# A two-layer graph kernel: two basis products in 15 block products, a root and an output product in seven

## The chip, the cores and the metric

The kernel runs on one core of a Trainium2 chip. The core has a matrix engine (TensorE, "PE" in the profile, with its weight loads as "PEld"), a vector engine (VectorE, "DVE"), an activation engine (ScalarE, "ACT"), a general engine (GpSimd, "POOL"), and queues that start transfers between main memory and the core's own memory (the one used most is that of SyncE, "SP"). Products land in PSUM, which has eight banks of 128 x 512 float32; VectorE and ScalarE read them from there. The metric is the device time of one execution in microseconds (us), as the median of the runs.

## The reference

Two graph blocks follow each other on 384 nodes with 1024 features. The first is an attention block with an edge mask; the change leaves it alone. The second is a relational convolution in two layers, with 768 features inside:

```python
h = relu(layernorm(x))                       # x is the output of the attention block
f = relu(h @ w_in + b_in)                    # 384 x 768
for l in range(2):
    W = einsum('rb,bio->rio', comp[l], basis[l])   # 6 relations out of 4 bases, 768 x 768 each
    h_all = einsum('ni,rio->rno', f, W)
    agg = segment_sum(h_all[edge_type, src] * norm[:, None], dst)   # mean by relation and node
    f = batchnorm(relu(agg + f @ root[l] + conv_bias[l]) + f)
x = x + layernorm(f @ w_out + b_out) * ln_gamma + ln_beta
```

The kernel writes the sum over edges as products with count matrices. With A_r the 384 x 384 matrix of relation r (counts divided by their sums), and At_b = sum over r of comp[r, b] A_r, a layer is: sum over b of At_b (f basis_b), plus f root, plus the bias.

## The kernel before

All matrices are float32, in tiles of 128 partitions. A float32 matmul shows as two instructions in the trace. The work of the second block runs in this order, and each step has a name in the profile.

- **Input product** (`ps_x`, `multiply`, L402): f = relu(h w_in), held as `XT`, six feature tiles by 384 nodes. It is done by a seven-product scheme (Winograd's form of Strassen's): the matrices are cut in quarters, VectorE makes four sums of each, and seven quarter products stand for eight. Every scheme named below works that way: fewer matmuls, paid with sums of operands and with results that are read out of PSUM and added.
- **Bases** (`ps_g`, L985 and L979, the loop over `b`): for every basis, H_b = f basis_b, 384 x 768. Node blocks 0 and 1 go by seven products, node block 2 directly. That is 33 matmuls with 384 columns, or 66 instructions. VectorE makes the sums of the weights (`weight_sums`, L927 and L929; `last_sums`, L935) and of f (`node_sums`, L920), ScalarE copies first results to `H`, and VectorE adds second ones (L992, L1000, L1002). The last product of a basis (`rest`) is issued inside the next.
- **Counts and mixes** (`share`, L361 to L367; `mix`, L346 and L348): GpSimd counts the edges into tables with indirect transfers (L283), loads them as `A` (L850 to L854) and adds them up (L355, L356). `share` makes a division by the sums, and `mix` forms `At`. A dictionary, `between`, fixes by (layer, basis, step) where these stand: in layer 0 at bases 2 and 3 and at the root, in layer 1 at its bases.
- **Root** (`ps_c`, L1019): f root, directly, 36 matmuls with 384 columns, accumulated in six banks to which the first mixed product is added.
- **Mixed product and normalisation** (`ps_c`, L1077): the sum over b of At_b H_b as seven-product schemes, in three pairs of feature tiles. For each pair VectorE makes four sums of `H` (`feature_sums`, L1097), adds seven results to `XN` (`take`, L1107), and makes the batch norm (`measure`, L1042 to L1049, `normalise_layer`, L1054 to L1058).
- **Output product** (`ps_f`, L1183): f w_out, directly, one node block after another. Then come the row norm (L1187 to L1195), the addition of x (L1197) and the store (L1198). GpSimd has by then added ln_beta to x (L1170).

The order on TensorE, VectorE, GpSimd, SP and, from the second product on, ScalarE is the order of the program, since all of these engines are scheduled by hand. Each engine takes its instructions strictly in that order, so an instruction that waits holds up those behind it. SP issues the loads of weights in that order too. Weights use five buffers in turn (`wpool`, 768 KB each): a load waits until the fifth load before it has been used up.

Of the kernel before, what the change touches and what calls it, by code (L numbers as in the profile page):

```python
# [10 lines left out]
F32 = mybir.dt.float32  # L11
# [6 lines left out]
P = 128  # L18
# [10 lines left out]
HC = DC // 2  # L29
HN = N // 2  # L30
# [14 lines left out]

BQ, BK, BV, BIQ, BIK, BIV, B_IN, CB, GAM, BET, NCOL = 0, 8, 16, 24, 32, 40, 48, 54, 66, 78, 90
# [5 lines left out]
def gnn_kernel(ctx: ExitStack, tc: tile.TileContext, out, x, edges, chunks, cols, rows, small,  # L52
               wq, wk, wv, wiq, wik, wiv, wo, w_in, basis, root, w_out):
# [299 lines left out]
    def add_up(r):  # L353
        sums[r] = late.tile([P, N], F32, tag="sum", name="sum", bufs=4)
        nc.gpsimd.tensor_tensor(sums[r], A[:, r, 0, :], A[:, r, 1, :], ALU.add)  # L355
        nc.gpsimd.tensor_tensor(sums[r], sums[r], A[:, r, 2, :], ALU.add)  # L356

    def share(r):
# [3 lines left out]
        rn = late.tile([P, N], F32, tag="rn", name="rn", bufs=2)  # L362
# [9 lines left out]
    with ExitStack() as inner:  # L372
# [263 lines left out]
        A = late.tile([P, R, NT, N], F32, tag="A", name="A")  # L636

# [93 lines left out]
        for g in range(STEPS + 1):  # L731
# [14 lines left out]
            if f + 2 == STEPS:  # L746
# [4 lines left out]
                w_first = [wload(basis[0, 0, part], (2, DC), "w_c") for part in range(3)]  # L751
                w_first += [wload(basis[0, 1, part], (2, DC), "w_c") for part in range(2)]
# [117 lines left out]
        node_sum(T, 4, h2T, T4)  # L870
        rest = lambda: None
        for p in range(3):
# [13 lines left out]
            add_up_quad(quads[0][0], pb)  # L886
            multiply(pc, s[:, 0], T[1], True)
# [8 lines left out]
            if p == 0:  # L896
                output_sums(a[2], S[0])

# [7 lines left out]
    with tc.tile_pool(name="conv", bufs=1) as cp:  # L906
# [7 lines left out]

        def node_sums(X):
            S = cp.tile([P, 4, 3, P], F32, tag="S", name="S")
            for i, a, b, op in ((0, block(X, 1, 0), block(X, 1, 1), ALU.add), (1, S[:, 0], block(X, 0, 0), ALU.subtract),
                                (2, block(X, 0, 0), block(X, 1, 0), ALU.subtract),
                                (3, block(X, 0, 1), S[:, 1], ALU.subtract)):
                nc.vector.tensor_tensor(S[:, i], a, b, op)  # L920
            return S

        def weight_sums(w):
            T13 = keep.tile([P, 3, 2, HC], F32, tag="hT", name="T13")
            T2 = keep.tile([P, 3, HC], F32, tag="mask8", name="T2")
            for c in range(3):
# [5 lines left out]
        def last_sums(w, T2):  # L932
            T4 = cp.tile([P, 3, HC], F32, tag="T4", name="T4")
# [4 lines left out]
        w_first = [w_first[:3], w_first[3:]]  # L938

        def load_basis(l, b):  # L940
            w = w_first.pop(0) if w_first else []
# [328 lines left out]
```

## Time and profile before

| what | value |
|---|---|
| time, median of 3 runs | 715.99 us (715.83 to 717.43) |
| the profiled execution's own time | 717.47 us |
| its span in the trace | 715.7 us |
| granted TensorE clock, mean | 0.995 |
| PE busy | 699.9 us, 98% |
| PEld busy | 527.9 us, 74% |
| DVE busy | 512.6 us, 72% |
| POOL busy | 308.1 us, 43% |
| ACT busy | 157.6 us, 22% |

The span runs from the first to the last instruction of the trace; some 1.8 us of the execution's own time lie around it. The busy share of PE is of a pipelined engine and says only that it is seldom without work. A group of the profile reads: line, engine, operation, output <- inputs, partitions x elements, count, then busy time and mean nanoseconds of one, then idle time of the engine before it and what ended it. In a list in order of time the columns are start, length and what ran.

### The profile page before, as it was taken

The numbers are of one execution on the slowest core, as the hardware profiler recorded it, in microseconds if no ns is written. First come the engines' busy times: TensorE is split into PE (matmuls) and PEld (weight loads), VectorE is DVE, ScalarE is ACT, GpSimd is POOL, SyncE is SP. The second block draws the span as 40 slices with busy tenths as digits, with TensorE's granted clock in tenths as the row PEclk, the third lists the DMA queues.
The fourth block names the chain that finished last, engine by engine and source line by source line (L and its number), as shares of the span: only waits on it lengthen the run. The fifth ranks groups of instructions, "written<-read, shape, count | busy, mean of one in ns | idle before, by whom it ended". The sixth has DMA issues, their size and how long they took to land.

```text
span 715.7 us, 9149 instructions
## 1 busy us (share of the span) xinstructions
PE 699.9 (98%) x3228; PEld 527.9 (74%) x3228; DVE 512.6 (72%) x1307; ACT 157.6 (22%) x360; POOL 308.1 (43%) x239
## 2 busy tenths in 40 slices
PE   8999999999999999999999999999999999999995
PEld 7759999999997444478985555558975555579943
DVE  5886697868886699787534279798878766507756
ACT  3211111111111577410221124202131111011100
POOL 1366777778687788687786542000000000120000
PEclk9999999999999999999999999999999999999999
DMA  8788787373562622733424994311104322700001
GB/s 303 267 279 264 228 250 212 80 243 67 203 209 43 177 2 1 221 44 45 89 0 103 250 288 153 133 44 45 45 0 133 102 69 94 308 1 1 1 30 59
DMA packets 69180, 91.04 MB, mean 127 GB/s; under 512 B 22940, under 2 KB 50688, under 8 KB 68750
## 3 DMA queue, kind: packets, MB, share of 16 engines
q1 hardware_dynamic: 46830, 78.45, 32.6%
q0 software_dynamic: 21296, 9.60, 10.8%
q10 hardware_dynamic: 1008, 2.41, 0.9%
q8 instruction: 25, 0.41, 0.2%
q14 instruction: 21, 0.17, 0.1%
HBM read 79.27 MB, written 11.16 MB: 126 GB/s over the span
## 4 chain that ended last, share of the span: by engine, by line
PE 87%; DVE 10%; ACT 2%; DMA 1%; issue 0%; DVEq 0%; ACTq 0%
PE ps_g L985 12%; PE ps_g L979 10%; PE ps_k L402 10%; PE ps_c L1077 10%; PE ps_v L402 8%; PE ps_q L420 6%; PE ps_q L402 5%; PE ps_f L1183 4%; DVE At L348 4%; PE ps_y L402 3%; PE ps_c L1019 3%; PE ps_x L402 3%; PE ps_o L707 2%; PE ps_s L662 2%; PE ps_pT L696 2%; PE ps_v L586 2%
## 5 line engine op out<-in xcount | busy, mean ns | idle before, releaser
L283 POOL DMA_INDIRECT atab<-count,at x99 | 166.3, 1679 | 44.2 <-issue 23.5
L278 POOL DMA_INDIRECT mtab<-m_val,at x99 | 103.4, 1045 | 57.6 <-issue 22.9
L1170 POOL TENSOR_TENSOR x_sb<-x_sb,room 128x1024 f32<-128x1024 f32 x3 | 7.0, 2348 | 188.9 <-DMA room<-in_rows 188.9
L348 DVE SCALAR_TENSOR_TENSOR At<-A,small_sb,At 128x1152 f32<-128x1152 f32 x40 | 53.6, 1414 | 0.0
L979 PE MATMUL ps_g<-T,S 128*128 128x384 f32 x144 | 49.1, 486 | 0.0
L985 PE MATMUL ps_g<-w_c,XN 128*128 128x384 f32 x144 | 47.7, 487 | 1.1 <-DVE XN L1107 1.1
L985 PE MATMUL ps_g<-w_c,XT 128*128 128x384 f32 x144 | 47.9, 486 | 0.0
L420 PE MATMUL ps_q<-hT,w_q 128*128 128x384 f32 (+1 forms) x160 | 43.4, 435 | 1.4 <-DVE hT L108 1.4
L985 PEld LDWEIGHTS ps_g<-w_c,XN 128*128 128x128 f32 x144 | 27.3, 190 | 20.2 <-DVE XN L1107 1.4
L979 PEld LDWEIGHTS ps_g<-T,S 128*128 128x128 f32 x144 | 27.3, 190 | 19.2 <-ACT H L991 0.4
L985 PEld LDWEIGHTS ps_g<-w_c,XT 128*128 128x128 f32 x144 | 27.3, 190 | 18.8
L420 PEld LDWEIGHTS ps_q<-hT,w_q 128*128 128x128 f32 x160 | 30.1, 200 | 14.1 <-ACT hT L101 1.7
L1077 PE MATMUL ps_c<-At,H 128*128 128x192 f32 x216 | 36.4, 326 | 0.0
L1077 PEld LDWEIGHTS ps_c<-At,H 128*128 128x128 f32 x216 | 35.4, 190 | 0.5
L402 PE MATMUL ps_k<-T,S 128*128 128x192 f32 x192 | 35.1, 326 | 0.0
L1107 DVE TENSOR_TENSOR XN<-XN,ps_c 128x192 f32<-128x192 f32 x38 | 12.5, 349 | 30.8 <-ACT XN L1063 19.7
L402 PEld LDWEIGHTS ps_k<-T,S 128*128 128x128 f32 x192 | 31.8, 190 | 0.0
L1183 PE MATMUL ps_f<-w_out,XN 128*128 128x512 f32 (+1 forms) x84 | 31.1, 531 | 0.0
L675 DVE CUSTOM_DVE_ANT_0 s<-ps_s,mask 128x384 f32<-128x384 f32 x48 | 24.5, 550 | 5.3 <-PE ps_s L662 5.3
L267 DVE SCALAR_TENSOR_TENSOR same<-cells,own,later 128x128 f32<-128x128 int32 x99 | 28.0, 350 | 0.4
L267 DVE SCALAR_TENSOR_TENSOR same<-keys,key,weigh 128x128 f32<-128x128 int32 x99 | 27.9, 349 | 0.0
L1183 PEld LDWEIGHTS ps_f<-w_out,XN 128*128 128x128 f32 x84 | 15.9, 190 | 14.9 <-issue 14.3
(298 smaller groups left out, 1411.6 us busy)
## 6 DMA issues: line engine op xcount, KB each, us to landing
w_c<-in_basis SPq DMA_DIRECT2D x96, 192.0 KB, 4.1
atab<-zero SPq DMA_DIRECT2D x36, 192.0 KB, 5.2
A<-atab POOLq DMA_DIRECT2D x12, 576.0 KB, 9.0
keys<-keys_d SPq DMA_DIRECT2D x25, 192.0 KB, 5.1
w_c<-in_root SPq DMA_DIRECT2D x6, 768.0 KB, 7.1
w_q<-in_wiq SPq DMA_DIRECT2D x16, 256.0 KB, 6.4
w_k<-in_wk SPq DMA_DIRECT2D x16, 256.0 KB, 5.8
w_k<-in_wik SPq DMA_DIRECT2D x16, 256.0 KB, 3.0
```

The source lines that it names most:

```text
L267: nc.vector.scalar_tensor_tensor(same, row[:, n, :], mine[:, c:c + 1], times, ALU.is_equal, ALU.mult, accum_out=count[:, i, c:c + 1])
L278: nc.gpsimd.indirect_dma_start(mtab[c // PER][:, :], bass.IndirectOffsetOnAxis(at[:, 0, c:c + 1], 0), m_val[:, c:c + 1], None)
L283: nc.gpsimd.indirect_dma_start(atab[0 if i < 11 else i % 2][:, :], bass.IndirectOffsetOnAxis(at[:, 1, c:c + 1], 0), count[:, 1, c:c + 1], ...
L348: nc.vector.scalar_tensor_tensor(At[:, b], A[:, r], w, At[:, b], ALU.mult, ALU.add)
L402: nc.tensor.matmul(ps, a[:, k, :], b[:, k, :], start=start and k == 0, stop=(k == 3), skip_group_check=not start)
L420: nc.tensor.matmul(ps[o][:, c], wt_[:, k, o * P:(o + 1) * P], src[:, k, c], start=(k == 0 and c.start == 0), stop=(k == KD - 1 and c.stop ...
L675: nc.vector.tensor_tensor_reduce(s[j], ps[:, :N], mask8[:, t, :], -scale, 3.0e38, ALU.add, ALU.min, tops[:, j:j + 1])
L979: nc.tensor.matmul(ps, x[:, c], y(c), start=start and c == 0, stop=(c == 2), skip_group_check=not start)
L985: nc.tensor.matmul(ps, block(XT, n, i)[:, c], w[c][:, i, o * HC:(o + 1) * HC], start=(first and c == 0), stop=(c == 2 and (i == 1 or ps is ...
L1019: nc.tensor.matmul(pr[o], w[k // 2][:, k % 2, o * P:(o + 1) * P], XT[:, k, :], start=(k == 0), stop=(k == KC - 1))
L1077: nc.tensor.matmul(ps, x[:, c], y[:, c], start=start and c == 0, stop=stop and c == 5, skip_group_check=True)
L1183: nc.tensor.matmul(p, XT[:, k, t * P:(t + 1) * P], w[k // 2][:, k % 2, c0:c1], start=(k == 0), stop=(k == KC - 1))
```

## The change

It has five parts.

1. **Bases 0 and 1 of layer 0** no longer go through the loop over `b`. `bases_by_15` cuts f in six blocks (three node blocks by two halves of the features) and the basis in six (two by three thirds of 256 outputs), and makes H with 15 block products where 18 would stand; a product is three matmuls with 256 columns. `X_SUMS` lists 11 sums of f, made once for both bases; `W_SUMS` lists 10 sums of each basis; `PRODUCTS` lists the order, the PSUM chain (0 to 3) on which a product accumulates, and the outputs to which the chain is put after it, with a sign. The first to reach an output is a ScalarE copy, later ones are VectorE additions. Sums stand some three products ahead of their use. The two bases are loaded in thirds (`thirds`), and room for sums is taken in `At`, `x_all`, `room2`, `mroom` and `w_room`.
2. **Sums for basis 2**: `weight_sums` of its parts 0 and 1 stand at the products 7 and 8 of basis 1, `node_sums` at its product 13, part 2 behind the last product. The loads stand at products 10 and 14 of basis 0 and 8 of basis 1.
3. **Root of layer 1** goes by seven products in three pairs of feature tiles (`second_root`), 63 matmuls with 192 columns. Its results go through PSUM to `XN` by ScalarE copies and VectorE additions, and the first mixed products are added from banks of their own. The sums of f stand at (1, 3, 1), the first sums of the root at (1, 3, 2).
4. **Output product**: node blocks 0 and 1 by seven products with 512 columns, block 2 directly as before. The sums of w_out stand ahead of the mixed product of layer 1 and inside its pairs (`out_sums`). `finish` makes the row norm; for block 0 and half of block 1 it uses ScalarE and GpSimd and stores from SP.
5. **The addition of ln_beta to x** moves from GpSimd at the end to VectorE in the input product, with a load on SP behind the first five loads of bases.

```diff
+W_SUMS = (
+    (6, 1, 2, 1, 5, -2),
+    (7, 1, 1, 1, 6, -1),
+    (8, 1, 4, 1, 7, 0),
...
+PRODUCTS = (
+    (2, 1, 0, ((4, 1),)),
+    (6, 6, 1, ((7, 1), (8, -1))),
+    (7, 7, 0, ((7, 1),)),
+    (5, 8, 2, ((7, 1),)),
+    (9, 9, 1, ((6, -1),)),
+    (10, 10, 0, ((8, -1),)),
+    (3, 4, 3, ((4, 1),)),
+    (11, 5, 0, ((5, -1),)),
+    (12, 12, 3, ((3, -1),)),
...
+                for b, t in ((0, 2), (0, 1), (0, 0), (1, 2), (1, 1)):
+                    load_third(b, t)
+                nc.sync.dma_start(boB, rows[R_LNB:R_LNB + 1, :].to_broadcast([P, D]))
...
+            for t in {1: (0,), 2: (1, 2)}.get(p, ()):
+                nc.vector.tensor_tensor(x_sb[:, t, :], x_sb[:, t, :], boB, ALU.add)
...
+        def bases_by_15():
+            todo = [(g * NPROD + w[5], 1, g, i) for g in range(BY_15) for i, w in enumerate(W_SUMS) if g or i > 1]
...
+            todo += [(first[x[0]] - 3, 2, 0, i) for i, x in enumerate(X_SUMS) if x[0] not in (6, 14)]
+            todo = sorted(todo + [(NPROD + 13, 3, 0, 0)] + [(NPROD + k, 4, 0, c) for c, k in enumerate((7, 8))])
+            for step in range(NPROD * BY_15):
+                g, k = step // NPROD, step % NPROD
+                while todo and todo[0][0] <= step:
+                    _, kind, *what = todo.pop(0)
+                    if kind == 1:
+                        sum_weights(*what)
+                    elif kind == 2:
+                        sum_features(what[1])
+                    elif kind == 3:
+                        third.append(node_sums(XT))
+                    else:
+                        third.append(weight_sums(basis_loads, what[1]))
...
+                for j in range(3):
+                    nc.tensor.matmul(ps, x[:, j], w[:, j], start=start and j == 0, stop=(j == 2),
+                                     skip_group_check=not start)
+                for to, sign in targets:
...
+                    if (g, to) in begun:
+                        nc.vector.tensor_tensor(dst, dst, ps, ALU.add if sign > 0 else ALU.subtract)
+                    elif sign > 0:
+                        nc.scalar.copy(dst, ps)
+                    else:
+                        nc.scalar.activation(dst, ps, AF.Identity, scale=-1.0)
...
+                if (g, k) == (0, 7):
+                    load_third(1, 0)
+                elif (g, k) in ((0, 10), (0, 14), (1, 8)):
+                    basis_loads.append(wload(basis[0, len(basis_loads)], (2, DC), "w_c"))
...
+        def second_root(rest):
+            root_w.append(wload(root_thirds[2], (KC, HC2), "w_c"))
...
+            shares_ = share_sums()
+            for p in range(3):
...
+                times(pa, root_block(p, 0, 0), x_quarter(0, 0), True)
+                nc.scalar.activation(quads[0][0], pa, AF.Identity, bias=bs[0])
+                rest()
+                times(pb, root_block(p, 0, 1), x_quarter(1, 0), True)
+                nc.vector.tensor_tensor(quads[0][0], quads[0][0], pb, ALU.add)
+                times(pc, s[:, 0], T[0], True)
+                nc.scalar.activation(quads[1][1], pc, AF.Identity, bias=bs[1])
+                if p < 2:
+                    root_S.append(root_sums(p + 1))
+                times(pa, s[:, 1], T[1])
...
+                w_end = [wload(w_out[part], (2, D), "w_out") for part in range(3)]
...
+                out_sums((0, 0), (1, 0), (0, 1), (1, 1))
...
             pa = first_of(0)
+            if l:
+                rest()
...
                 times(pa, S[p][1], T2)
                 take(o0, 1, pa)
                 next(sums, None)
+                if l + 1 == L:
+                    out_sums(*(((0, 2), (1, 2), (2, 2), (3, 2)) if last else ((2, p),)))
                 times(pc, S[p][3], q(1, 1))
...
                 ready = measure(rectify(o1))
                 pa = following
+                if l + 1 == L:
+                    out_sums((3, p))
...
-        for t in range(NT):
-            nc.gpsimd.tensor_tensor(x_sb[:, t, :], x_sb[:, t, :], rowsB[:, 2, :], ALU.add)
...
+        third(*parts[0], 0, 1)
+        times(pa, block(XT, 0, 0), b_end(0, 0), True)
+        put_out(0, 0, pa, True, False)
+        times(pb, block(XT, 0, 1), b_end(1, 0), True)
+        put_out(0, 0, pb, False, True)
+        times(pc, OS[0], summed(0), True)
...
+        times(pa, OS[2], summed(2))
+        finish(0)
+        put_out(1, 0, pa, False, True)
+        put_out(1, 512, pa, False, True)
+        third(*parts[0], *range(2, KC))
+        for p, c0 in parts[1:]:
+            third(p, c0, *range(KC))
+        finish(1)
+        for p, c0 in parts:
+            put_out(2, c0, p, True, True)
+        finish(2)
```

## The prediction

> **What bounds the kernel now.** I read the page's shares first, then the chain that ended last in order of time, then the costs by shape, then single stretches of VectorE.
>
> ```profile
> PE 699.9 (98%) x3228; PEld 527.9 (74%) x3228; DVE 512.6 (72%) x1307; ACT 157.6 (22%) x360; POOL 308.1 (43%) x239
> PEclk9999999999999999999999999999999999999999
> ```
>
> TensorE is hardly ever without work, at a granted clock of 0.995. Only fewer or shorter matmuls, or the ends of the span, can bring time.
>
> ```profile
> 332.45 3.45 PE ps_y L840 x16
> 341.11 2.60 PE ps_x L402 x16
> 368.91 0.37 DVE XT L882
> 370.89 11.61 PE ps_g L985 x36
> 459.46 26.58 DVE At L348 x20
> 616.99 19.35 PE ps_c L1019 x60
> 677.29 30.94 PE ps_f L1183 x84
> 708.26 0.43 DVE hf L1187
> ```
>
> The chain is PE nearly throughout, so its pieces give the price of a matmul instruction: 384 columns 11.61/36 = 0.3225 us, 256 columns 3.45/16 = 0.2156, 192 columns 2.60/16 = 0.1625. The output product is 60 instructions with 512 columns and 24 with 256: (30.94 - 24 x 0.2156)/60 = 0.4295. Per column that is 0.838 to 0.846 ns, so narrower matmuls lose nothing here. One stretch of the chain is VectorE's: the mixes of layer 0 (26.58 us).
>
> **What TensorE saves.** A float32 matmul is two instructions.
> - Bases 0 and 1: before 2 x 66 x 0.3225 = 42.57 us; after 2 x 15 x 3 x 2 = 180 x 0.2156 = 38.81. Saves 3.76.
> - Root of layer 1: before 72 x 0.3225 = 23.22; after 3 x 7 x 3 x 2 = 126 x 0.1625 = 20.48. Saves 2.74. The four first mixed products remain.
> - Output: before 30.94; after 7 x 3 x 2 = 42 x 0.4295 = 18.04 and block 2 as before, 12 x 0.4295 + 24 x 0.2156 = 10.33. Saves 2.57.
>
> Together 9.07 us. The rest of the working is how much of that VectorE takes back.
>
> **Bases 0 and 1.**
>
> ```profile
> L927 DVE TENSOR_TENSOR T<-w_c 128x768 f32<-128x768 f32 x15 | 14.3, 952 | 0.0
> L929 DVE TENSOR_TENSOR T<-w_c,T 128x384 f32<-128x384 f32 x15 | 8.4, 558 | 0.5
> L1187 DVE TENSOR_TENSOR hf<-ps_f,room 128x256 f32<-128x256 f32 x2 | 0.8, 424 | 2.8 <-PE ps_f L1183 2.8
> ```
>
> A sum of weights has 768 elements (0.95 us; 0.87 from start to start where nothing depends on the one before), a sum of f 384 (0.56; 0.47), an addition out of PSUM 256 (0.42). In the 30 products VectorE has 18 sums of weights (two stand earlier), 9 of f, 20 additions, and for basis 2 two weight parts of 1.46 us and four node sums (2 us): 18 x 0.92 + 9 x 0.50 + 20 x 0.40 + 2.9 + 2 = 34 us, against 38.8 of PE. Nearly full, so order decides. I laid both queues side by side from 370.9, product by product (1.29 us each), with 0.15 us from a product's end to its reader. All sums are in time by 1.5 us or more, since they stand three products ahead. Late are the banks: the sums of steps 4 to 6 (three of weights, three of f, 4.3 us) stand in front of the additions of products 5 and 6, while product 7 needs the bank of 5, and product 8 that of 6. PE stands 0.36 and 0.55 us. In the second basis, with no sums of f, it doesn't stand. All at the short spacings the loss is 0.5, all at full lengths 1.7; I take 0.9, between them.
>
> **GpSimd beside it.** It is still counting until 386, and VectorE now works through that stretch. The Trainium skill, "SBUF — State Buffer", section "SBUF: two separate sides", says that a VectorE instruction with two SBUF inputs and a GpSimd instruction that reads SBUF exclude each other for a whole instruction.
>
> ```profile
> 373.38 0.95 DVE L927 TENSOR_TENSOR T<-w_c 128x768 f32<-128x768 f32 x1
> 374.37 0.56 DVE L929 TENSOR_TENSOR T<-w_c,T 128x384 f32<-128x384 f32 x1
> 374.73 1.63 POOL L283 DMA_INDIRECT atab<-count,at  x1 [0.31 <-issue]
> 376.66 2.02 POOL L283 DMA_INDIRECT atab<-count,at  x1 [0.30 <-issue]
> ```
>
> By the rule VectorE would lose up to the 12.6 us that GpSimd is busy from 371.3 to 386. The rows show VectorE at its usual 0.95 and 0.56 inside that stretch, and GpSimd stretched: five counts from 370.66 to 381.00 take 2.07 us each, 1.86 elsewhere. I take the row. VectorE loses nothing; GpSimd's last eight counts come some 1.7 us later, and `A` with them. The sums of relations 0 to 5 were ready at 404.4 to 435.4, and the earliest `share` now stands at about 414.5 (was 417.16), the last at about 443 (was 446.46): still hidden, by at least 4 us.
>
> **Transfers.**
>
> ```profile
> 390.00:411.00 21.00, 21.00 (x66) 12.35 (x65) 7.44 (x12) 2.87 (x6) 9.68 (x10) 1.00 0.96 274
> 411.00:434.00 23.00, 23.00 (x73) 13.46 (x72) 18.36 (x18) 6.05 (x12) 12.22 (x12) 1.00 1.05 264
> ```
>
> The last two columns are the DMA share and GB/s: here the loads of `A` fill the DMA engines. Part 1 of basis 2 is loaded into the buffer that product 14 of basis 0 frees, at about 391.6, and VectorE asks for it at 402.3. Beside the loads of `A`, a part of weights came 7.5 us (freed 388.1, used 395.68) and 9.3 us (409.4, 418.74) after its buffer was free, so it lands at 399 to 401. PE would feel it from about 404 on, then microsecond for microsecond, since the sums and additions of basis 1 wait behind it. Cost nothing, with little room. Part 2 may land after 411, but only T4 and the first `share` stand behind it.
>
> From basis 2 on, layer 0 is what it was, earlier: the last additions of basis 3, the 26.6 us of mixes behind them and PE's 1.1 us wait before 495.17 all move along. The ln_beta additions (3 x 1.2 us) and four early sums lie in VectorE's gaps of 2.3 to 4.9 us during the input product; its load of 0.5 MB is issued at 343, used at 356. Nothing. GpSimd's additions that go away ended at 631, hidden too.
>
> **Root of layer 1.** Sums of f (4 x 0.69) and of the root (4 x 0.5) join basis 3, where VectorE stood 6.3 us. In the root, a pair is 6.83 us of PE and at most 5.8 of VectorE (three additions of 0.35, four sums, two of the `At` sums of 1.35). Once, in the second pair, `rest` waits for an addition behind such a sum: 0.2 us. Its third part of weights, asked for some 9 us after its buffer is free, is there. Behind the root stand the last `At` sums, four sums of w_out (0.61 each from start to start, between 0.47 and 0.87) and the first feature sums, about 8.5 us; PE has 8.8 us of mixed products meanwhile. Nothing.
>
> **Mixed product of layer 1.** Here a cover is thin.
>
> ```profile
> 659.89 0.95 DVE L1097 TENSOR_TENSOR room<-H 128x768 f32<-128x768 f32 x1
> 660.76 0.35 DVE L1107 TENSOR_TENSOR XN<-XN,ps_c 128x192 f32<-128x192 f32 x1
> ...
> 671.64 0.35 DVE L1107 TENSOR_TENSOR XN<-XN,ps_c 128x192 f32<-128x192 f32 x1
> 673.42 0.35 DVE L1107 TENSOR_TENSOR XN<-XN,ps_c 128x192 f32<-128x192 f32 x1 [1.44 <-PE ps_c L1077]
> ...
> 681.57 0.48 DVE L1058 TENSOR_SCALAR XN<-XN,sc 128x384 f32<-128x384 f32 x1
> ```
>
> The second pair takes PE 11.7 us and VectorE as long; the addition at 660.76 frees its bank at 661.1, and PE writes there again at 661.5. Two sums of w_out for each of the first two pairs add 1.2 us a pair. Laid out like the bases (the same layout of the kernel before gives no wait, and the last normalisation 4.8 us after the last product, as in the trace), PE waits 0.4 and 0.3 us in pair 1 and 0.8 in pair 2: 1.5, or 2.1 with full lengths. In the last pair four sums (2.45 us) stand ahead of the addition of 673.42, whose gap takes 1.44. So the last normalisation ends 6.6 to 6.9 us after the last product. PE can work until then on two feature tiles of block 2 (4 x 0.43), one product (6 x 0.43) and two thirds of the next (4 x 0.43), 6.0 us; before it had 16 x 0.43 = 6.9 us for 4.8. It waits 0.7.
>
> **Output and end.** The four node sums (2 us) and the additions (0.69, with statistics 1.45) fit behind the products (2.58 us each). Block 2's 8.6 us of PE cover the end of block 1, about 5.6 us of VectorE. The end from the last matmul on is the same 7.4 us. The six GpSimd instructions of `finish` (1.3 us each at L355's rate) end before it; if one did hold VectorE there, it would cost up to 1.3.
>
> **Sum.** -9.07 + 0.9 + 0.2 + 1.5 + 0.7 = -5.8 us. On the profiled execution (717.47 us, span 715.7) that gives 711.7 and 709.9; the median lies 1.5 us below that execution, so the time is 715.99 - 5.8 = 710.2 us. A kernel of this length tells a change from none from about 0.3% on, 2.1 us.
>
> **Rivals.**
> - *VectorE keeps up everywhere*, because sums overlap more than I let them: 715.99 - 9.07 = 706.9 us. For it: the nearest rows of two-input sums run 0.08 us closer than their length. Against it: the thin covers above. 0.12.
> - *The transfer decides.* Part 1 of basis 2 lands 13.6 us after its buffer is free, as the loads issued between 412 and 420 did (median to landing): 405.2, which costs 1.3 us by the layout, 711.5; at 17 us it costs 4.7, 714.9. Against it: the loads of basis 2 now start earlier, so fewer compete. 0.18, at about 712.5.
> - *Slower: VectorE is locked out by GpSimd* as the rule says, from 371 to 386. It has 0.5 us of slack, so nearly all of 12.6 us goes to PE: 710.2 + 12 = 722. It makes the kernel slower than before once more than 5.8 us, some half of GpSimd's busy time, really blocks. Against it are the rows above. 0.08.
> - The sum as it stands: 0.62, with 708.8 to 711.9 as its own range (bases 0.5 to 1.7, pairs and their end 1.5 to 3.1, the end 0 to 1.3).
>
> The range of 707.0 to 714.6 leaves out half of the first rival, a quarter of the second and the slower one, 0.19. Faster by over 0.3% (below 713.8) are the sum, the first rival and two thirds of the second, 0.85; within it 0.07; slower 0.08.
>
> **What would show it.** `ps_g` in bases 0 and 1: 180 instructions in 38.8 us, and PE idle about 1 us near 380 and 381.5, released by VectorE's additions to `H`. Basis 2 starts near 410.6; the mixes of layer 0 start 2.8 us earlier, at 456.6. The root of layer 1 is 126 instructions. In its mixed product PE waits for L1107's successor, in all about 1.5 us, and the output product waits 0.7 us for the last normalisation. I am wrong if PE idles by many microseconds in the bases (behind VectorE or a load), if layer 0's mixes do not start earlier, or if the output product waits for VectorE's additions.

## The result and the profile after

| what | before | changed |
|---|---|---|
| median of 22 runs each, same chip | 716.06 us (715.83 to 717.73) | 712.61 us (709.96 to 717.87) |
| ratio of the two, 95% interval | | 0.995 (0.9931 to 0.9968) |
| the profiled execution's own time | 717.47 us | 709.97 us |
| its span, granted clock | 715.7 us, 0.995 | 708.2 us, 0.996 |

The kernel became faster by 0.5% in the median, inside the range of the prediction (707.0 to 714.6) and 2.4 us above its 710.2. The spread is the unexpected part. The kernel before took 715.9 or about 717.5 us and little else. The changed one took 709.96 to 710.71 us in nine of 22 executions, and anything up to 717.87 in the others. A ratio compares only the executions of both kernels that are least disturbed, so that below it can even point the other way than the medians (run 2). Two questions follow: whether the sum of the prediction is right, which is read from an execution of the first kind, and what takes the gain away in the others.

The shares and the granted clock, from the page of the changed kernel:

```profile
PE 691.4 (98%) x3324; PEld 541.1 (76%) x3324; DVE 557.9 (79%) x1381; ACT 162.9 (23%) x375; POOL 313.5 (44%) x242
PEclk9999999999999999999999999999999999999998
```

PE has 8.5 us less to do and VectorE 45.3 us more; PE is still seldom without work.

The chain that ended last, in order of time (start, length, what ran):

```profile
369.31 10.36 PE ps_g L1095 x48
379.70 19.71 PE ps_g L1095 x90
...
400.85 8.14 DMA w_c<-in_basis
409.04 4.14 PE ps_g L1245 x12
...
455.32 26.58 DVE At L398 x20
...
677.88 14.00 PE ps_f L1492 x32
691.89 8.63 PE ps_f L1503 x32
```

The stretches are those of before, with three stretches of PE shorter: the bases (L1095), the root of layer 1 (L1183) and the output product (L1492, L1503). A new link stands between bases 1 and 2: the product at 409.04 follows a load that landed at 409.00 by this view. An addition of VectorE ended at 408.98, so that the two arrive together there; which of them counts, runs 7 and 12 show below.

Where PE waits in the new parts, from its instructions in order of time (the bracket is the idle time before and what ended it):

```profile
409.04 4.14 PE L1245 MATMUL ps_g<-w_c,XT 128*128 128x384 f32 x12 [0.58 <-DVE H L1101]
665.50 2.22 PE L1348 MATMUL ps_c<-At,room 128*128 128x192 f32 x12 [0.16 <-DVE XN L1375]
677.88 1.13 PE L1492 MATMUL ps_f<-w_out,XN 128*128 128x512 f32 x2 [0.26 <-DVE XN L1333]
```

To compare executions I count from the first matmul of basis 0 (`ps_g`), because what lies ahead of it is the same work in both kernels. The marks are the first count matmul (`ps_cnt`, one product into basis 2), the start of the root of layer 1, the start of the output product and the end of the span.

| us from the first base matmul | start of bases | first count | root of layer 1 | output | end |
|---|---|---|---|---|---|
| before | 370.72 | 46.44 | 240.30 | 306.40 | 344.98 |
| changed | 369.15 | 43.86 | 237.72 | 302.31 | 339.05 |
| difference of the parts | -1.57 | -2.58 | 0.00 | -1.51 | -1.84 |

The part that the change touches is 5.93 us shorter; the forecast was 5.8. The remaining 1.57 us lie ahead of it: the clock granted in the first 60 us was 0.97 in the profile before, where it was half from 12.7 to 16.1 us, and 1.00 in this one.

### The profile page after: what moved, and what is told of

The parts are those of the page before. It is cut to its first block, busy times and chain, and to the rows that moved or that the text cites. A ratio compares the mean times of both kernels' runs of the same rounds, so it can differ in the third digit from the quotient of the medians.

```text
span 708.2 us, 9470 instructions
## 1 busy us (share of the span) xinstructions
PE 691.4 (98%) x3324; PEld 541.1 (76%) x3324; DVE 557.9 (79%) x1381; ACT 162.9 (23%) x375; POOL 313.5 (44%) x242
## 3 DMA queue, kind: packets, MB, share of 16 engines
q0 software_dynamic: 21296, 9.60, 10.6%
## 4 chain that ended last, share of the span: by engine, by line
PE 81%; DVE 13%; ACT 2%; DMA 2%; issue 1%; SPq 0%; DVEq 0%; ACTq 0%
PE ps_k L452 10%; PE ps_g L1245 9%; PE ps_v L452 9%; PE ps_g L1239 8%; PE ps_c L1348 7%; PE ps_q L470 6%; PE ps_q L452 5%; PE ps_g L1095 4%; DVE At L398 4%; PE ps_y L452 3%; PE ps_x L452 3%; PE ps_c L1183 3%; PE ps_o L758 2%; PE ps_s L713 2%; PE ps_pT L747 2%; PE ps_v L636 2%
## 5 line engine op out<-in xcount | busy, mean ns | idle before, releaser
L1478 POOL TENSOR_TENSOR hf<-hf,room 128x512 f32<-128x512 f32 x3 | 4.3, 1421 | 257.8 <-ACT hf L1476 257.8
L470 PE MATMUL ps_q<-hT,w_q 128*128 128x384 f32 (+1 forms) x160 | 41.8, 422 | 1.4 <-ACT hT L151 1.4
L470 PEld LDWEIGHTS ps_q<-hT,w_q 128*128 128x128 f32 x160 | 28.5, 190 | 14.1 <-ACT hT L151 1.7
L1348 PE MATMUL ps_c<-At,H 128*128 128x192 f32 x216 | 36.7, 326 | 0.0
L1348 PEld LDWEIGHTS ps_c<-At,H 128*128 128x128 f32 x216 | 35.3, 190 | 0.5 <-DVE XN L1375 0.2
L1239 PE MATMUL ps_g<-room,x_all 128*128 128x384 f32 x72 | 25.2, 486 | 0.0
L1245 PE MATMUL ps_g<-w_c,XT 128*128 128x384 f32 x72 | 24.3, 487 | 0.6 <-DVE H L1101 0.6
L1282 PE MATMUL ps_c<-XT,w_c 128*128 128x384 f32 x72 | 23.5, 486 | 0.0
L758 PE MATMUL ps_o<-At,v 128*64 128x384 f32 x96 | 20.8, 512 | 1.3 <-ACT attT L761 1.3
L713 PE MATMUL ps_s<-k,q 64*128 64x384 f32 x96 | 21.5, 528 | 0.0
L1245 PEld LDWEIGHTS ps_g<-w_c,XT 128*128 128x128 f32 x72 | 13.6, 190 | 10.3 <-DVE H L1101 1.0
L1239 PEld LDWEIGHTS ps_g<-room,x_all 128*128 128x128 f32 x72 | 13.7, 190 | 9.5
```

The source lines that it names most:

```text
L470: nc.tensor.matmul(ps[o][:, c], wt_[:, k, o * P:(o + 1) * P], src[:, k, c], start=(k == 0 and c.start == 0), stop=(k == KD - 1 and c.stop ...
L713: nc.tensor.matmul(score[g][j][:, :N], q2[ho, hc, t * P:(t + 1) * P], k2[ho, hc, :], start=True, stop=True)
L758: nc.tensor.matmul(pso[p][j * HD:(j + 1) * HD, :N], v2[:, m, h * HD:(h + 1) * HD], turned(g)[:, j, :], start=(m == 0), stop=(m == NT - 1))
L1239: nc.tensor.matmul(ps, x[:, c], y(c), start=start and c == 0, stop=(c == 2), skip_group_check=not start)
L1245: nc.tensor.matmul(ps, block(XT, n, i)[:, c], w[c][:, i, o * HC:(o + 1) * HC], start=(first and c == 0), stop=(c == 2 and (i == 1 or ps is ...
L1348: nc.tensor.matmul(ps, x[:, c], y[:, c], start=start and c == 0, stop=stop and c == 5, skip_group_check=True)
```

## The experiments

They are numbered as their labels are; none has the number 11. They ran on three chips. On the first two (runs 1 to 4, and 5 to 8) both kernels are longer and spread widely. The profile of the kernel before on the second of them, run 5, shows why: its bases start at 381.59 us instead of 370.72, with PE waiting 4.1 us for `issue` and 3.5 us for ScalarE in the projections (`ps_k`). From the first base matmul to the end it takes 345.01 us there, and 344.98 in the profile on which the prediction rests. So the stages, counted from that matmul, can be compared between chips, and the medians only between kernels that ran side by side.

**The whole change again (1), and its pieces (2 to 4).** Run 1 is the changed kernel. Run 2 puts the weight sums of basis 2 behind basis 1:

```diff
-            todo = sorted(todo + [(NPROD + 13, 3, 0, 0)] + [(NPROD + k, 4, 0, c) for c, k in enumerate((7, 8))])
+            todo = sorted(todo + [(NPROD + 13, 3, 0, 0)])
...
-                S, T = third[-1], weight_sums(w, 2)
+                S, T = third[-1], weight_sums(w)
```

Run 3 takes bases 0 and 1 back to the loop and keeps root and output in seven; run 4 keeps the bases in 15 and takes root and output back (of both edits the main lines):

```diff
...
-                bases_by_15()
-                w = load_basis(0, BY_15)
-                S, T = third[-1], weight_sums(w, 2)
-            for b in range(0 if l else BY_15, B):
+                S = node_sums(XT)
+                w = load_basis(0, 0)
+                T = weight_sums(w)
+            for b in range(B):
```

```diff
...
-            if l:
-                rest = second_root(rest)
-            else:
-                w = [wload(root[part], (2, DC), "w_c") for part in range(3)]
...
+            w = [wload(root[l, part], (2, DC), "w_c") for part in range(3)]
```

> The changed kernel once more, as it is. Its executions lay between 709.96 and 717.87 us, nine of 22 within 0.5 us of 710.3, while those of the kernel before lie at 715.9 or 717.5. Theory (transfer): in the long executions a part of basis 2 lands late beside the loads of A, VectorE stands before the sums that stand at products 7 and 8 of basis 1, and PE loses that time before basis 2; a profile of a long execution then shows PE idle of 2 to 7 us in bases 0 and 1, ended by a VectorE addition or sum, with VectorE waiting for w_c. Rival (counts): GpSimd's tables come late and PE waits at a share. Rival (clock): no PE idle, but matmuls of the same shape get longer, with a granted clock under 1.00 somewhere. Time: median 710 to 714, with a spread of several us.

> The weight sums of basis 2 stand behind basis 1 instead of at its products 7 and 8; the loads are where they were. Transfer theory: a late load no longer stands before the sums and additions of basis 1, and basis 2 itself needs the sums only 13 us later. The spread goes away, all executions lie at 710 to 711.5 us. Counts and clock rivals: the spread stays as in the changed kernel, 710 to 718.

> Bases 0 and 1 go through the loop as before, root and output product stay in seven. By the prediction's sum: -2.74 - 2.57 + 0.2 + 1.5 + 0.7 = -2.9 us, 713.1 us. Transfer theory and counts rival: no spread beyond that of the kernel before, 713.0 to 714.8. Clock rival, if the denser work at the end is its cause: the spread stays.

> Only bases 0 and 1 in 15 products with the moved sums of basis 2 (and the ln_beta addition), root and output product as before. By the prediction's sum: -3.76 + 0.9 = -2.9 us, 713.1 us in the shortest executions. Transfer theory and counts rival: the spread is all here, 713 to 721, median about 715.5. Clock rival: no spread if the end is its cause.

Measured, with the kernel before at 750.44 us on this chip (728.33 to 762.12, 17 runs):

| run | median us | ratio (95%) | first count | root to output | output to end | end |
|---|---|---|---|---|---|---|
| 1 changed | 737.13 (6 runs) | 0.9838 (0.9771 to 0.9906) | 45.37 | 64.58 | 36.70 | 340.51 |
| 2 sums behind | 742.24 (12 runs) | 1.0124 (1.0057 to 1.0192) | 44.53 | 64.58 | 36.68 | 339.65 |
| 3 bases back | 747.63 (6 runs) | no interval | 46.44 | 64.57 | 36.70 | 343.33 |
| 4 bases only | 743.55 (6 runs) | 0.9877 (0.9793 to 0.9961) | 45.18 | 66.11 | 38.35 | 343.49 |

Medians and ratios decide nothing here: the range of the kernel before is 34 us wide. So what was expected of the spread, in run 2 above all, could not be judged on this chip. The stages are clear. Root and output give the same 1.53 and 1.88 us with and without the bases (before 66.10 and 38.58). Taken back, the root gives nothing, and of the end 0.23 us remain, behind the last matmul. In run 3 the total falls by only 1.65, since PE waits once for a bank that ScalarE still has to read:

```profile
PE ps_g L1232 <- ACT H L1244: 1.5, 1, 1.5
```

It stands in basis 2, which all these kernels compute in the loop. The trace tells where it comes from: VectorE waited there for a part of the weights that landed 1.5 us later than in the kernel before (49.50 us behind the first base matmul, before 48.02). Its three last sums of weights then took 3.09 us, where the kernel before took 1.49, beside two additions of `A` on GpSimd (1.24 and 1.20 us). The division of `share` behind them came 3.1 us late, and ScalarE's copies behind that 1.8. The first count is the part that varies: 45.37 in run 1, 45.18 in run 4, 44.53 in run 2, 43.86 in the first profile.

**The node sums and the additions of GpSimd (5 to 7).** Run 5 is the kernel before, unchanged, run 6 the changed kernel. In run 6, VectorE's and GpSimd's instructions just ahead of basis 2, and PE's:

```profile
419.74 0.55 DVE L1027 TENSOR_TENSOR x_all<-XT 128x384 f32<-128x384 f32 x1
420.20 2.58 DVE L1027 TENSOR_TENSOR x_all<-XT,x_all 128x384 f32<-128x384 f32 x1
422.71 0.41 DVE L1101 TENSOR_TENSOR H<-H,ps_g 128x256 f32<-128x256 f32 x1
...
420.85 1.51 POOL L405 TENSOR_TENSOR sum_room<-A 128x384 f32<-128x384 f32 x1
422.44 1.20 POOL L406 TENSOR_TENSOR sum_room<-sum_room,A 128x384 f32<-128x384 f32 x1
...
423.17 4.14 PE L1245 MATMUL ps_g<-w_c,XT 128*128 128x384 f32 x12 [2.61 <-DVE H L1101]
```

A node sum that takes 0.55 us takes 2.58 beside two additions of `A` on GpSimd. It stands in front of the last addition to `H`, whose bank the first product of basis 2 needs, and PE waits 2.61 us (2.10 in run 1, 2.17 in run 8). Run 7 moves the node sums behind that addition:

```diff
-            todo = sorted(todo + [(NPROD + 13, 3, 0, 0)] + [(NPROD + k, 4, 0, c) for c, k in enumerate((7, 8))])
+            todo = sorted(todo + [(NPROD + k, 4, 0, c) for c, k in enumerate((7, 8))])
...
-                S, T = third[-1], weight_sums(w, 2)
+                S, T = node_sums(XT), weight_sums(w, 2)
```

> The kernel before, for its stage lengths on the chip of this call. From the first base matmul to the end of the span it took 344.98 us; all theories expect 344.9 to 345.1 here, whatever the whole time is, if that part of the program is as even as it looks. If the whole time is over 716, the extra lies before the first base matmul (370.7 on the profile before).

> The changed kernel again. From the first base matmul to the end 339.05 us in its profile. Theory (early part): executions differ before the first base matmul, in the projections of the attention block, which the change doesn't touch: PE waits there for sums of weights that come late, and matmuls behind such a wait are longer for a while. The part from the first base matmul on lies at 339.0 to 340.6, the difference being GpSimd's additions that stop VectorE ahead of basis 2. Rival (transfer in the bases): a long execution has 2 to 7 us of PE idle in bases 0 and 1, behind w_c.

> The node sums for basis 2 stand behind the last addition of basis 1, not ahead of it. The changed kernel's profile has PE wait 0.58 us before basis 2 for that addition, and 2.10 us where two GpSimd additions (1.52 and 1.20 us) stretched two node sums from 0.56 to 1.40 and 1.23. Theory (the last addition is held up by node sums, and they by GpSimd): the wait goes away, the first count matmul comes 43.3 us after the first base matmul (43.86 and 45.37 in the changed kernel), and the part from there to the end is 338.5 in either case. Rival (part 2 of basis 2 lands late): no change.

Measured beside a kernel before of 729.73 us (722.53 to 741.66, 17 runs): run 5 728.35 us in one execution. Run 6 721.2 us (718.3 to 735.67, 12 runs), ratio 0.9904 (0.9864 to 0.9944), first count at 45.88, end at 341.03, a little over what was expected. Run 7 717.9 us (715.43 to 733.43, 4 runs), ratio 0.9868 (0.9799 to 0.9936), first count at 43.77, end at 338.87. The node sums are stretched in run 7 too (1.24 and 1.34 us), but no longer in front of an addition. PE still stood 0.51 us, because the first product of basis 2 takes the bank of the very last addition. That wait was not foreseen, and run 12 removes it.

**Sums of w_out on GpSimd (8 and 9).** The 12 sums of the output product go to GpSimd, which is idle by then, ahead of the mixed product of layer 1:

```diff
-                        nc.vector.tensor_tensor(out_T[i][:, c], x(c), y(c), ALU.subtract)
+                        nc.gpsimd.tensor_tensor(out_T[i][:, c], x(c), y(c), ALU.subtract)
...
-                out_sums((0, 0), (1, 0), (0, 1), (1, 1))
+                out_sums(*((i, c) for c in range(3) for i in range(4)))
```

In run 8 the fourth kind of sums overwrites an operand of the root's last product, so its result and its time are not those of the idea. Run 9 issues three kinds there, and the fourth behind that product:

```diff
+                out_sums(*((i, c) for c in range(3) for i in range(3)))
...
                 rest()
+                out_sums(*((3, c) for c in range(3)))
```

> All twelve sums of w_out on GpSimd, ahead of the mixed product of layer 1, none on VectorE. In the changed kernel the stretch from the first root matmul of layer 1 to the output product takes 64.59 us (63.36 of matmuls: 66.10 - 2.74) and PE then waits 0.26 for the last normalisation. Theory by the count rows (VectorE isn't stopped by GpSimd): the waits of that stretch fall from 1.2 to 0.2 us and the 0.26 goes away, 1.2 us less in all. Theory by the additions of A (a GpSimd instruction with SBUF inputs stops a VectorE one with two SBUF inputs): GpSimd's 12 x 1.42 = 17 us stretch VectorE's feature sums and additions to about twice their length in the first pair and a half; VectorE is up to 5 us late there and PE waits 2 to 5 us, so 64.6 to 68.

> All sums of w_out on GpSimd, now with the fourth kind behind the last root product, whose sums it overwrites. Theory (a GpSimd instruction with SBUF inputs stops a VectorE one with two SBUF inputs, seen where the additions of A meet node sums): VectorE's feature sums and additions beside GpSimd's 17 us stretch by up to 1.4 us each, PE waits 2 to 5 us in the first pair and a half, and the stretch from the first root matmul of layer 1 to the output product is 65 to 68 us (64.59 in the changed kernel). Rival (GpSimd stops nothing): 63.4 to 63.6, and no wait for the last normalisation.

Run 8: 739.16 us (734.67 to 742.05, 4 runs), ratio 1.0158 (1.009 to 1.0225). PE's waits in its root and mixed product, in all, times, longest:

```profile
PE ps_c L1183 <- POOL sum_room L1308: 12.2, 2, 8.1
```

This is one mistake of order and no measure of GpSimd. Run 9, one execution on the last chip: 710.35 us, root to output 65.25 us (64.59 in the changed kernel), output to end 36.16 (36.74), end at 339.15 (339.05). Taking 12 sums off VectorE gained nothing, and this is why, in run 9:

```profile
637.82 5.16 POOL L1308 TENSOR_TENSOR sum_room<-w_out,x_all 128x512 f32<-128x512 f32 x3
...
638.60 2.02 DVE L1365 TENSOR_TENSOR room<-H,room 128x768 f32<-128x768 f32 x1
...
649.96 0.95 DVE L1365 TENSOR_TENSOR room<-H,room 128x768 f32<-128x768 f32 x1
```

The sum of `H` that takes VectorE 0.95 us alone takes 2.02 beside them. What VectorE is relieved of, it loses in waiting: in the 65.1 us from 606.9 on, it is busy for 48.41 us with 12 sums fewer, and 47.62 in the changed kernel. PE waited 1.9 us in all from root to output (65.25 less 63.36 of matmuls), 1.2 in the changed kernel.

**Without GpSimd's additions (10).** The count matmul adds up three node blocks of `A` itself, and GpSimd adds nothing:

```diff
-        nc.gpsimd.tensor_tensor(sums[r], A[:, r, 0, :], A[:, r, 1, :], ALU.add)
-        nc.gpsimd.tensor_tensor(sums[r], sums[r], A[:, r, 2, :], ALU.add)
...
-        nc.tensor.matmul(ps[:, :N], ones, sums[r], start=True, stop=True)
+        for c in range(NT):
+            nc.tensor.matmul(ps[:, :N], ones, A[:, r, c, :], start=(c == 0), stop=(c == NT - 1))
```

> The changed kernel without GpSimd's additions of A: TensorE sums the three node blocks of a relation in the count matmul, 12 more matmuls or 7.7 us of PE, all from basis 2 on. Theory: with no GpSimd instruction beside them no VectorE sum of bases 0 and 1 is longer than 0.97 us, node sums are 0.56 each, PE waits 0.5 to 0.6 us before basis 2, and the first count matmul comes 43.8 us after the first base matmul (43.86 in the profile of the changed kernel, 45.37 and 45.88 in the two later ones, where GpSimd's additions met the node sums). Rival (late weights hold up VectorE): 44 to 46 here too. The part from the first base matmul to the end: 339.05 + 7.7 = 346.8.

One execution: 719.21 us, first count at 43.87, end at 346.66. The end is 7.61 us later than in the changed kernel, which is the price of 24 more instructions of 384 columns (24 x 0.3225 = 7.74). The bases are as in the best executions: VectorE's sums take 0.95 and 0.55 us throughout, 1.01 at most, and PE waits 0.58 us ahead of basis 2. So without GpSimd's additions nothing is stretched; but since this was one execution, and the additions cost nothing in the first profile either, it bounds their cost and doesn't measure it.

**A better order (12), beside the changed kernel (13).** Run 12 is run 7 with the bank of the last addition moved to the end of the ring, so that basis 2 takes it last:

```diff
+            last = chain[1, 0][1]
+            ring.remove(last)
+            ring.append(last)
```

> The node sums behind the last addition of basis 1, as in the earlier run, where PE still waited 0.51 us: the first matmul of basis 2 takes the bank that the last addition reads. Here the banks are turned by one so that it takes another. Expected: no wait, first count matmul 43.3 us after the first base matmul, first base matmul to the end 338.4 us; against the changed kernel 0.6 to 2.6 us less. Whole time by the chip's own early part.

> The changed kernel beside the improved one. First base matmul to the end 339.0 to 341.1 us. If the early part (up to the first base matmul) is as even on this chip as where the kernel before ran at 715.83 to 717.73, all its executions lie within 2 us; else the spread is that of the kernel before on the same chip.

On this chip the kernel before takes 716.04 us (715.65 to 718.89, 23 runs).

| run | median us | ratio (95%) | first count | end |
|---|---|---|---|---|
| 12 node sums and bank | 711.91 (710.18 to 717.23, 12 runs) | 0.9952 (0.9931 to 0.9973) | 43.00 | 338.10 |
| 13 changed | 716.53 (710.71 to 718.3, 12 runs) | 0.9994 (0.9974 to 1.0013) | 43.85 | 344.31 |

In run 12 the wait ahead of basis 2 is gone. Its PE, at the end of basis 1 and the start of basis 2:

```profile
408.64 1.46 PE L1095 MATMUL ps_g<-w_c,At 128*128 128x256 f32 x6
409.93 4.03 PE L1248 MATMUL ps_g<-w_c,XT 128*128 128x384 f32 x12
```

The start follows by the usual 1.29 us of a product, and the end is 0.95 us earlier than in the changed kernel. The lowest times of both (710.18 and 709.96) don't show it, for the profiled execution of run 12 had a clock of 0.97 in its first 60 us and started its bases at 370.80.

Run 13 is the most telling one. On a chip like the first, the changed kernel, exactly as it was, now shows no gain over the kernel before, and the profile is of a long execution, 718.12 us. The end at 344.31 lies outside what was expected (339.0 to 341.1). Its bases are as good as ever (43.85). The loss comes behind them. PE in order of time, with the second `share`:

```profile
416.48 4.03 PE L1245 MATMUL ps_g<-w_c,XT 128*128 128x384 f32 x12
423.92 0.91 PE L411 MATMUL ps_cnt<-sum_room,ones 128*128 128x384 f32 x2 [3.40 <-POOL sum_room L406]
424.67 5.73 PE L1245 MATMUL ps_g<-w_c,XT 128*128 128x384 f32 x12
430.23 0.81 PE L411 MATMUL ps_cnt<-sum_room,ones 128*128 128x384 f32 x2
```

PE stands 3.40 us for a sum of `A`, and then the next twelve instructions take 5.73 us instead of 4.03. The stretches of the same execution give the granted clock (stretch, its length, busy time of PE, PEld, DVE, ACT and POOL with their instructions, then PEclk, DMA share and GB/s):

```profile
420.38:423.92 3.54, 0.14 (x2) 0.00 (x1) 1.48 (x2) 0.00 (x0) 3.46 (x5) 1.00 0.83 141
425.00:426.00 1.00, 1.00 (x3) 0.52 (x2) 0.00 (x0) 0.97 (x2) 1.00 (x3) 0.57 0.96 387
426.00:427.00 1.00, 1.00 (x3) 0.59 (x2) 0.87 (x1) 0.10 (x1) 0.92 (x2) 0.50 1.03 197
427.00:428.00 1.00, 1.00 (x2) 0.43 (x2) 1.00 (x1) 0.00 (x0) 0.97 (x1) 0.50 1.08 195
430.30:432.00 1.70, 1.70 (x7) 1.04 (x6) 0.00 (x0) 0.89 (x2) 0.96 (x1) 1.00 0.98 248
```

From 425.1 to 428.6 the clock is half. The wait thus costs 3.40 + 1.70 = 5.10 of the 5.26 us that this execution lies behind the first profile from the bases on. The other 2.84 us lie ahead of the bases, which start at 371.99: the clock of the first 60 us was 0.94, with half the clock from 12.1 to 19.0 us.

Why the sum was late shows in the chain that ended last in run 13, which leads from this count matmul back to GpSimd's sums, its loads of `A` and its counts. Two transfers of that chain, of a count and of a load:

```profile
393.65 3.50 DMA atab<-count,at
...
406.52 12.41 DMA A<-atab
```

GpSimd's own order there:

```profile
396.71 1.56 POOL L333 DMA_INDIRECT atab<-count,at  x1 [1.23 <-DMA atab<-count,at]
397.80 2.14 POOL L907 DMA_DIRECT2D A<-atab  x2
...
419.22 1.30 POOL L909 DMA_DIRECT2D A<-atab  x1 [4.42 <-DMA A<-atab]
420.03 1.29 POOL L911 DMA_DIRECT2D A<-atab  x1
420.82 1.97 POOL L405 TENSOR_TENSOR sum_room<-A 128x384 f32<-128x384 f32 x1
422.87 0.99 POOL L406 TENSOR_TENSOR sum_room<-sum_room,A 128x384 f32<-128x384 f32 x1
```

The first load of `A` follows the last count, 25.8 us after the start of the bases (397.80 - 371.99). In the first profile of the changed kernel that is 20.7 us, and 15.7 in the kernel before. From there to the second sum it takes 26.1 us, 25.0 in the first profile and 25.2 in the kernel before. So run 13 lost its cover ahead of the first load, in the counts. What is left to each `share`, as the time between the end of a sum on GpSimd and PE's count matmul:

| us of cover | first load of A, after the bases' start | share 1 | share 2 | share 3 | share 4 |
|---|---|---|---|---|---|
| before | 15.7 | 12.8 | 10.1 | 9.2 | 10.6 |
| changed, first profile | 20.7 | 8.1 | 2.7 | 0.5 | 4.9 |
| changed, run 13 | 25.8 | 1.0 | -3.4 | 2.3 | 5.5 |

So one execution has 0.5 us to spare and another lacks 3.4.

## Why the prediction was right, and where it wasn't

The sum came out in the undisturbed execution, 5.93 us for 5.8, if not term by term. That the median lies in the range is owed to its width: the executions that put it 2.4 us above 710.2 lose time for which the sum had no term.

**Savings of PE.** Right. `ps_g` in bases 0 and 1 is 180 instructions, the root of layer 1 126, the output 42 with 512 columns in block 0 and 1; a product of six follows the next by 1.29 us.

**Bases, +0.9.** The size held, the place didn't. The first count lies 38.81 + 3.87 = 42.68 us behind the start if PE never stands; it was 43.86, so 1.18 us were lost where 0.9 were given. The two bank waits of 0.36 and 0.55 us were forecast near 380 and 381.5; all 30 products together lost 0.43. The other 0.75 stands between 407.00 + 1.29 and 409.04: the first product of basis 2 takes the bank that the last addition of basis 1 frees. The layout of the prediction ended with the last product and let that bank be free. Run 7, with the node sums out of the way, still waits 0.51 us there; run 12, with another bank, doesn't wait. So the bank is the cause, and node sums that GpSimd stretches make it longer (2.61 us in run 6).

**GpSimd beside it.** The rule of the Trainium skill, "SBUF — State Buffer", section "SBUF: two separate sides", was set aside because of rows of counting, and for counting the rows were right. VectorE in the changed kernel, while GpSimd counts:

```profile
372.16 0.95 DVE L939 TENSOR_TENSOR room<-w_c 128x768 f32<-128x768 f32 x1
373.03 0.55 DVE L941 TENSOR_TENSOR At<-XT 128x384 f32<-128x384 f32 x1
...
372.91 1.63 POOL L333 DMA_INDIRECT atab<-count,at  x1 [0.30 <-issue]
```

Beside GpSimd's additions the rows agree with the rule. The same profile, 30 us later:

```profile
402.26 1.75 DVE L943 SCALAR_TENSOR_TENSOR w_room<-w_c,x_all 128x768 f32<-128x768 f32 x1
...
411.04 1.33 DVE L1036 TENSOR_TENSOR mroom<-w_c,room 128x384 f32<-128x384 f32 x1
...
403.28 1.60 POOL L406 TENSOR_TENSOR sum_room<-sum_room,A 128x384 f32<-128x384 f32 x1
...
412.04 1.52 POOL L405 TENSOR_TENSOR sum_room<-A 128x384 f32<-128x384 f32 x1
```

0.95 has become 1.75 and 0.56 has become 1.33, and GpSimd's own additions are longer too (1.60 and 1.52, 0.99 without company). The prediction looked at the counts only and passed over these additions, which the change brings beside VectorE's fullest stretch. In the first profile they hit sums that had time; in run 6 they hit the node sums, and PE waited 2.61 us in place of some 0.6.

**`A` "still hidden, by at least 4 us".** This is the step that failed; in the one long execution that was traced it cost 5.1 of the 5.9 us gained. It had two terms. The first: GpSimd's last eight counts were to come 1.7 us later. From the start of the first of them to the first load of `A` they took 19.4 us in place of 15.8, and they began 1.3 us later against the start of the bases, so that this load stood 5.0 us later. That they get longer is no chance: it is 15.6 to 15.8 us in the three profiles with these bases in the loop (before, runs 3 and 5), and 16.2 to 19.5 in the eleven others. Two of the eight waited for the transfer of an earlier count:

```profile
378.26 2.01 POOL L333 DMA_INDIRECT atab<-count,at  x1 [1.86 <-DMA atab<-count,at]
...
386.20 1.55 POOL L333 DMA_INDIRECT atab<-count,at  x1 [1.93 <-DMA atab<-count,at]
```

The second wait falls into 268 GB/s of weight loads (382 to 385), which the change issues from 379.71 on; the kernel before moved 2 GB/s from 370 to 386. The first wait has no such company (0 GB/s from 376 to 379), and its cause is open. The second term was that a sum, once late, would be late by the same amount further on. In the first profile the four sums were 2.1, 4.8, 6.2 and 3.2 us later than before, counted from the bases' start. With shares some 2.6 us earlier, as forecast, the cover of 9 to 13 us went down to 0.5 to 8, not to "at least 4".

What the prediction left out is how much the start of the counts moves from one execution to the next. The last 37 counts ahead of those eight take 79.3 to 81.8 us in all 14 profiles, whatever PE does meanwhile. The first of them began 79.4 us ahead of the bases in the profile before and in the first profile of the changed kernel, but 73.7 us in run 13, and 73.6 and 75.2 in runs 10 and 9. So in run 13 the first load of `A` stood 10.1 us later than before: 5.7 for the start of those 37 counts, 1.9 for their length, 2.5 for the last eight. Of 10.1 us of cover for share 2 that leaves nothing; the share itself stood 2.6 us earlier and the stretch from load to sum was 0.9 longer, which makes the 3.4 us of waiting.

**Root and mixed product of layer 1, +1.7.** Mis-sized: from the root to the output the part fell by 1.51, not 1.04, so the waits were 1.23 us. The first pairs' waits were drawn too long; the only idle of PE at L1348 in the profile's list is 0.16 us.

**Last normalisation, 0.7.** Too large: it ended at 677.83, 6.2 us after the last mixed product (671.62), where 6.6 to 6.9 were given, and PE idled 0.26 us for it. That the part from output to end still fell by 1.84 (forecast 2.57 - 0.7 = 1.87) is in part luck. From its first to its last matmul the output product fell by 2.05, from 31.09 to 29.04 us, and the end behind it, forecast as the same, grew by 0.2, from 7.47 to 7.68 us.

**Transfers and the rivals.** In the first profile and in run 13, the two ends of the spread, the waits of PE in bases 0 and 1 and at the start of basis 2 are put down to VectorE's additions alone. One load of basis 2 landed 0.02 us behind such an addition (409.00 and 408.98), 9.6 us after its buffer was free (399.40), where the prediction had 7.5 to 9.3. So the loads arrive just in time, as was said, and a faster basis 1 would meet them next. The transfer rival's time of 712.5 was met by the median, but not for its reason. VectorE did not keep up everywhere (706.9), and a loss of 12 us to GpSimd did not come (722). The addition of ln_beta costs PE nothing: from the first matmul of the input product to the first of the bases both kernels take 29.78 us. From the first count to the root of layer 1 both take 193.86.

**What stays open.** Only one long execution was traced. That the others, between 712 and 718 us, lose by late shares and by the clock of the first 60 us fits most of their granted clocks (0.990 to 0.995 in run 13, 0.997 in its only one of 710.71 us), but was not seen. Five of the first 22, from 713.06 to 715.29 us, have 0.996, as the one of 709.97 has: there 3 to 5 us went without a loss of clock, so if it was a wait for a sum, the clock was not halved behind it. Nor is it shown what delays the counts more than 70 us ahead of the bases. A kernel with later shares or earlier counts, which would settle it, was not tried. Whether run 12's lower median, 711.91 beside 716.53, comes from its edit or from fewer late counts is open too: its third share had 0.4 us of cover.

## What to carry to other kernels

When an edit speeds up one engine, list what the neighbours hand to it (here the sums of `A`, which come from counts, transfers and GpSimd's additions) and shorten each cover by the whole distance by which the use moves forward and the producer back; a cover that is smaller than the producer's own variation shows as a spread of times before it shows in a profile. Put sums that only the next stage needs behind the additions that free its banks, and give the bank that comes free last to the product that comes last. Before work is moved to an idle GpSimd, look whether VectorE is then running sums of two inputs: 12 sums moved there gained nothing (one execution).

## What the runs showed of the hardware

- **A wait of PE can halve the clock of the matmuls behind it for 3.4 us.** After the 3.40 us of run 13, twelve instructions took 5.73 us instead of 4.03, at half the clock from 425.1 to 428.6. How long a wait has to be for that, these runs do not settle. After 2.61 us in run 6 the next twelve took 4.14 us, at a clock of 1.00; after 2.17 us at the same place in run 8 they took 5.83, at half the clock from 421.3 to 424.7:

```profile
420.32 5.83 PE L1245 MATMUL ps_g<-w_c,XT 128*128 128x384 f32 x12 [2.17 <-DVE H L1101]
```

  The Trainium skill, "TensorE: Matmul & The Clock Gate", section "HAM oscillation — how this bites in real kernels", names gaps of more than about 3.4 us; here a shorter one did it too. So a late operand can cost 1.7 us more than its wait, and a wait of 2 us is no safe one.
- **The mean clock of the first 60 us takes three levels**, 1.00, 0.97 and 0.94: none, 3.4 or 6.8 us of them ran at half the clock. In profiles on chips where the kernel before takes 716 us, the bases start at 369.2, 370.7 to 370.8 and 372.0 us with them. The kernel before was seen at the first two levels (run 5 and its first profile); the two starts are as far apart as its two times, 715.9 and 717.5.
- **GpSimd's additions and its counts differ for VectorE**: beside additions a sum of two inputs takes up to 2.58 us for 0.55, beside counts it takes its usual time. The counts themselves get longer when the bases go by 15 products (16.2 to 19.5 us for the last eight, up to the first load, in place of 15.6 to 15.8); by what, is not shown.
